# A quarter of the gate products moved from VectorE to ScalarE and GpSimd, with a new order of the experts' halves and own tables for one unit

## The chip, the core and the metric

The kernel runs on one core of a Trainium2 chip. A core has TensorE (PE: matmuls, with a weight load PEld that overlaps them), VectorE (DVE), ScalarE (ACT), GpSimd (POOL) and SyncE (SP, which issues DMAs). Each engine executes its own instructions in order; engines wait for one another by semaphores. The metric is the device time of one execution in microseconds (us). Before the change it is 1290.98 us, the median of 3 runs (1289.37 to 1291.66).

## The reference, cut to what matters

The input is 2 batches of 1024 tokens of 128 values. Four blocks are each added to the residual:

```
x = x + attention+MLP, 2 layers      (block 1)
x = x + local attention+MLP, 2 layers (block 2)
x = x + local and latent attention   (block 3)
x = x + experts(layernorm(x))        (stage D)
```

Block 2 has 8 heads of 64. Queries and keys are l2-normed, scaled, and rotated with per-position tables: `q * cos * scale + rotate_half(q) * sin * scale`, and for k with the inverse scale. The kernel holds the products of the position tables with the learned scales in tiles `tab`.

Stage D has 64 experts of 32 hidden values, all computed for all 2048 tokens, and a routing that masks the scores:

```
scores = softmax(x @ Wr + br)                  # 2048 x 64
order  = argsort(-scores, axis=0)              # tokens of each expert
group  = sorted.reshape(32, 64, 64).sum(1)     # sums of 64 ranks
mask   = the 512 best of the 2048 groups, put back in token order
fs     = where(mask, scores, 0) / (sum + 1e-6)
h      = silu(x @ Wup + bup) * (x @ Wgate + bgate) * fs
out    = h @ Wdown + fs @ bdown
```

## The kernel before

All four stages run in one program. In blocks 1 to 3 and stage D the order of PE, ACT, DVE and POOL instructions is written by hand: each engine gets its instructions as the Python code emits them. Blocks 1 and 2 use a `Pipe`: `later(n, f, rank)` puts `f` n beats ahead, and within a beat the lower rank comes first.

**Block 2** (`BlockB`) has 32 units (2 layers, 2 batches, 8 tiles of 128 positions), one in every 8 beats. A unit projects q and k to PSUM (`queries`, L714) and v (L719), squares and sums (L723, L736), takes the root (`root`, L742), and scales q and k into the tile `raw` (`scale`, DVE, L748 to L752). On POOL follow `cross` (L761: two products of the swapped halves with the sine table, into `t2`) and `straight` (L768: the product with the cosine table, in place); `both` adds them (L775, on POOL, but on DVE for the first unit). Transposes on PE and copies on ACT make `qT` and `kT` (L807, L809), and the scores follow (L822), their maximum, exponential, product with v, and a quarter-wise MLP.

The first unit's opening steps (`clear`, `turn`, `copy`, `queries`, `square`, `sums`, `root`, `scale`) are handed to block 1 (`first`, L554), whose last group of tokens emits them among its own work (`BlockA.after`, L425). Block 2's pools reuse the memory of block 1's pools. The scale-and-position tables of all 8 tiles are built by `tables` on POOL: for layer 0 the four parts for tiles 0 to 3 in beat 0 with the rank -2, those for tiles 4 to 7 from beat 20 on; they take their tiles from block 2's pool `b2`. Block 1's tile `hid` (512 hidden values of its MLP) is in its pool `a1`. The input norm of the following 512 tokens (`prep`, `norm`: statistics on DVE L641, root on POOL L645 to L648, product on ACT L652) is set for beat 6 for the first of them.

**Stage D.** The 64 experts give 32 units of 128 hidden rows x 512 tokens x 2, so 64 halves. A half is: the up matmul (128x512, `matmul`, L1652, into a PSUM bank `big`), a silu on ACT (L1661) into `hid`, the gate matmul (L1652), and on DVE one operation `hid = (gate + bias) * hid` (L1675), here called the gate. `Experts` keeps lists of ups and of gates to be made and a queue `ready` of gates whose matmul is emitted. `feed` keeps 3 gates in `ready` (4 once no up is left), `fill(n)` retires n gates, and after each emits one up and feeds. The last two halves' `hid` lies in the expert input `xT` itself (L1645).

`route` computes the mask on DVE and calls `fill` between its steps, so that matmuls, silus and gates run beside it: 

- 36 items of sort passes over parts of the scores that block 3 left over (`front.todo`); up to two gates in three items, one in two at the end
- ten passes over 1024 values, each a max and a min (L1511, L1512), with one gate after each
- the exchange of the two batches' halves through two DMAs, one issued by SP, one by ACT (L1841, L1842), with four gates and two subtractions (L1816) while they run; L1848 takes what they bring
- four passes, a gate after each; then the sign (L1858), the sums of 64 (L1862), their broadcast to all partitions by 16 PE transposes and 4 ACT copies (L1869, L1870), a minimum (L1871), three gates
- five rounds of a search (L1883 to L1895; the compare of 2048 values with a running sum is L1886), one gate in each
- the tail: four short chains that go DVE, PE, DVE (L1904, L1917, L1937, L1947) with three gates beside each, two compares over all scores (L1961, L1962), the rest of the gates, and the scan (L1969)

After the scan come the masks and the down matmuls (L1727), which need all halves.

Of the kernel before, what the change touches and what calls it, by code (L numbers as in the profile page):

```python
# [28 lines left out]
P = 128  # L29
# [3 lines left out]
MT = S // P  # L33
# [144 lines left out]
class BlockA:  # L178
# [11 lines left out]
    def __init__(self, k, es, nxt):  # L190
# [4 lines left out]
        self.p3 = es.enter_context(k.tc.tile_pool(name="a3", bufs=3))  # L195
        self.pipe = Pipe()
# [228 lines left out]
    def after(self, l, b, g, st):  # L425
# [6 lines left out]
        hid = self.p1.tile([P, 4, 512], F32, tag="hid", name=k.name("hid"))  # L432
# [106 lines left out]
class BlockB:  # L539
# [14 lines left out]
    def first(self):  # L554

        out = self.out = {}
        out["clear"], out["turn"], out["copy"] = self.features(0, 0, 0)
# [18 lines left out]
    def run(self):  # L576
        pipe = self.pipe
        self.tables(0)
        for n in range(1, 4):
            pipe.later(32 * n - (26 if n == 1 else 32), lambda n=n: self.prep(0, n % 2, n // 2, 1))  # L580
# [31 lines left out]
    def tables(self, l):  # L612
# [3 lines left out]
        for i, n in ((1, "b_qksr"), (0, "b_qks")):  # L616
            dst = self.p2.tile([P, MT, 2, 64], F32, tag=f"tab{i}", name=k.name("tab"))
            for j in range(2):
                for m in (slice(0, MT), ) if l else (slice(0, 4), slice(4, MT)):
                    sc = k.row(n, (l * 2 + j) * 64, 64)[:, None, :].to_broadcast([P, m.stop - m.start, 64])  # L620
                    self.pipe.later(
                        (2 if l else 5 * m.start) + 2 * j + 4 * (1 - i) if l or m.start else 0,
                        lambda dst=dst, i=i, j=j, m=m, sc=sc: nc.gpsimd.tensor_tensor(
                            dst[:, m, j, :], k.b_tab[:, m, 2 * i + j, :], sc, ALU.mult
                        ),
                        rank=3 if l or m.start else -2,
                    )
            out.append(dst)
        self.tabs[l] = out[::-1]

# [73 lines left out]
    def project(self, l, b, m, later):  # L704
        k, nc, st = self.k, self.k.nc, self.st[l][b]
        first = (l, b, m) == (0, 0, 0)
        t = st.setdefault("first", {}) if first else {}

# [48 lines left out]
        def cross():  # L757
            t2 = t["t2"] = self.p2.tile([P, 2, 8, 64], F32, tag="t2", bufs=1, name=k.name("t2"))
            r4 = t["raw"].rearrange("p (j h) d -> p j h d", j=2)
            for a, z in ((0, 32), (32, 0)):  # L760
                nc.gpsimd.tensor_tensor(  # L761
                    t2[:, :, :, a : a + 32], r4[:, :, :, z : z + 32],
                    self.tabs[l][1][:, m, :, None, a : a + 32].to_broadcast([P, 2, 8, 32]), ALU.mult,
                )

        def straight():
            r4 = t["raw"].rearrange("p (j h) d -> p j h d", j=2)
            nc.gpsimd.tensor_tensor(  # L768
                r4, r4, self.tabs[l][0][:, m, :, None, :].to_broadcast([P, 2, 8, 64]), ALU.mult
# [845 lines left out]
class Experts:  # L1615
# [39 lines left out]
    def up(self, n=1):  # L1655

        now = [(unit, e, self.matmul(unit, e, self.k.d_up)) for unit, e in self.ups[:n]]
# [8 lines left out]
    def feed(self):  # L1666

        while self.gates and len(self.ready) < (3 if self.ups else 4):
            unit, e = self.gates.pop(0)
            while (unit, e) in self.ups:  # L1670
# [3 lines left out]
            self.ready.append(  # L1674
                lambda ps=ps, hd=hd, bias=bias: self.k.nc.vector.scalar_tensor_tensor(  # L1675
                    hd, ps, bias, hd, ALU.add, ALU.mult
                )
            )

    def fill(self, n=1):  # L1680

        for _ in range(n):
            if self.ready:
                self.ready.pop(0)()
                self.up()
                self.feed()
# [109 lines left out]
def route(k, p1, front, fill):  # L1796
# [25 lines left out]
    for n, f in enumerate(front.todo):  # L1822
# [6 lines left out]
        fill(n % 2 if left < 10 else n % 3 > 0)  # L1829
# [395 lines left out]
```

## Time and profile before

| quantity | value |
| --- | --- |
| median of 3 runs | 1290.98 us |
| profiled execution | 1289.73 us, span 1287.9 us, mean clock 0.97 |
| block 1 | 0 to 341.8 us |
| first scores of block 2 (L822) | 357.29 us |
| stage D: last block of passes handed over, to the start of the ten long passes | 1067.60 to 1118.85 us |
| ten long passes and exchange, to L1848 | 1118.85 to 1142.04 us |
| merge and sums, to the first L1886 | 1142.04 to 1156.30 us |
| search, to L1894 | 1156.30 to 1173.57 us |
| tail, to the scan | 1173.57 to 1193.78 us |
| scan, masks, down matmuls | 1193.78 to 1287.9 us |

How to read the profile. It is one execution. The first lines give busy time and share of each engine; "the chain that ended last" follows the last instruction back through what released it. A row of a timeline has the start, the duration, the engine, the line of the kernel, the operation, `out<-in`, the tile's shape, the count of merged records, and in brackets the idle time of the engine before it with what ended that. A DVE row can last a little longer than the distance to the next row: instructions overlap at their ends, so what one costs in a chain is that distance, the slot. A 128x512 float32 matmul leaves two records. Windows give each engine's busy time in a stretch, with the clock that TensorE was granted.

### The profile page before, as it was taken

Reading aid. Unit: us, or ns where it says so; the run is one execution under the profiler, and the core shown is the slowest. Engines: PE = TensorE matmul, PEld = TensorE weight load, DVE = VectorE, ACT = ScalarE, POOL = GpSimd, SP = SyncE. Lnnn points to the kernel's source line nnn. Section 1 sums busy time; section 2 is a strip of 40 time slices with the busy share of each in tenths; the row PEclk is TensorE's granted clock in tenths of the full one; section 3 lists DMA queues with packets and bytes.
Section 4 is the critical chain, followed back from the end, with each engine's and each line's share of the span. In section 5 each row is a group of like instructions: output and inputs, shape, how many; then the busy total and the mean of one; then the engine's idle time right before and its main releaser. Section 6 shows DMA issues by size and latency. Waiting matters only on the chain.

```text
span 1287.9 us, 23417 instructions
## 1 busy us (share of the span) xinstructions
PE 1142.3 (89%) x9381; PEld 738.6 (57%) x9441; DVE 867.5 (67%) x1789; ACT 642.8 (50%) x1209; POOL 478.8 (37%) x556
## 2 busy tenths in 40 slices
PE   5899999999578999999989867989998978998798
PEld 3566666666345666666666634555555543343688
DVE  5566666554477776776776625556568989998763
ACT  5454545444355765665655635656766754342000
POOL 2523333232488786676786542212122210000000
PEclk9999999999899999999999988989999989999799
DMA  9000000000001100010100002000000000000000
GB/s 297 1 1 1 1 1 1 2 1 1 17 18 26 27 22 18 22 26 18 26 22 18 5 16 103 2 1 2 2 1 1 2 1 1 0 17 0 25 17 18
DMA packets 19841, 25.18 MB, mean 20 GB/s; under 512 B 2762, under 2 KB 13716, under 8 KB 19476
## 3 DMA queue, kind: packets, MB, share of 16 engines
q1 hardware_dynamic: 19076, 23.02, 6.3%
q8 instruction: 75, 1.23, 0.4%
q10 hardware_dynamic: 656, 0.66, 0.2%
q14 instruction: 34, 0.28, 0.1%
HBM read 13.32 MB, written 1.05 MB: 11 GB/s over the span
## 4 chain that ended last, share of the span: by engine, by line
PE 39%; DVE 20%; ACT 7%; issue 4%; POOL 3%; DVEq 0%; POOLq 0%; ACTq 0%
PE mm L1727 5%; PE bank L947 4%; PE big L1652 4%; PE s L714 3%; PE s L822 3%; PE s L1249 2%; PE bank L867 2%; PE tr L1286 2%; DVE nm L1254 2%; DVE r_zab L1511 2%; DVE r_zab L1512 2%; PE s L1245 2%; DVE hid L1675 2%; DVE rinv L736 2%; PE bank L964 1%
## 5 line engine op out<-in xcount | busy, mean ns | idle before, releaser
L1254 DVE TENSOR_REDUCE nm<-s 128x4 f32<-128x1024 f32 (+1 forms) x64 | 71.0, 1151 | 59.1 <-PE s L1249 59.0
L377 DVE TENSOR_REDUCE nm<-s 128x1 f32<-128x1024 f32 x64 | 75.1, 1215 | 51.7 <-PE s L371 51.7
L761 POOL TENSOR_TENSOR t<-raw,tab 128x512 f32<-128x512 f32 x64 | 79.7, 1268 | 77.1 <-DVE raw L752 73.0
L1287 ACT COPY pT<-tr 128x512 f32<-128x512 f32 x120 | 70.0, 598 | 69.5 <-PE tr L1286 69.2
L1661 ACT ACTIVATE hid<-big,cols 128x512 f32<-128x512 f32 x62 | 42.0, 687 | 75.6 <-PE big L1652 75.5
L1286 PE MATMUL tr<-ident,pr 128*128 128x128 f32 x480 | 77.6, 285 | 2.2 <-ACT pT L1287 1.8
L768 POOL TENSOR_TENSOR raw<-raw,tab 128x1024 f32<-128x1024 f32 x32 | 75.5, 2360 | 2.4
L723 ACT ACTIVATE sq<-s 128x1024 f32<-128x1024 f32 x32 | 32.8, 1025 | 85.7 <-PE s L714 85.7
L383 ACT ACTIVATE pr<-s,nm 128x1024 f32<-128x1024 f32 x64 | 71.1, 1122 | 7.7 <-DVE nm L377 7.6
L775 POOL TENSOR_TENSOR raw<-raw,t 128x1024 f32<-128x1024 f32 x31 | 73.3, 2365 | 1.7
L394 PEld LDWEIGHTS bank<-ident,pr 128*128 128x128 f32 x512 | 56.2, 141 | 30.0 <-issue 22.5
L406 PE MATMUL bank<-pT,v 128*64 128x128 f32 x1024 | 72.5, 286 | 0.7 <-DVE pT L399 0.2
L1652 PE MATMUL big<-xTd,d_gate 128*128 128x512 f32 x128 | 66.2, 609 | 7.7 <-DVE hid L1675 3.9
L1652 PE MATMUL big<-xTd,d_up 128*128 128x512 f32 x128 | 68.7, 627 | 2.3 <-DVE r_above L1891 2.3
L406 PEld LDWEIGHTS bank<-pT,v 128*64 128x64 f32 x1024 | 57.2, 141 | 22.4 <-issue 11.4
L397 ACT COPY pT<-bank 128x512 f32<-128x512 f32 x64 | 34.9, 588 | 68.2 <-PE bank L394 68.2
L1286 PEld LDWEIGHTS tr<-ident,pr 128*128 128x128 f32 x480 | 54.9, 145 | 20.8 <-issue 11.5
L371 PE MATMUL s<-kk,q 64*128 64x512 f32 x256 | 64.7, 615 | 0.6 <-ACT pr L383 0.5
L394 PE MATMUL bank<-ident,pr 128*128 128x128 f32 x512 | 65.2, 276 | 0.0
L714 PE MATMUL s<-b_wqkv,hT 128*128 128x512 f32 x128 | 63.8, 622 | 1.3 <-ACT hT L682 1.3
L1727 PEld LDWEIGHTS mm<-d_down,hid 128*128 128x128 f32 x496 | 60.4, 194 | 5.7 <-DVE xo L1758 1.9
L1727 PE MATMUL mm<-d_down,hid 128*128 128x128 f32 x496 | 61.1, 278 | 1.3 <-DVE xo L1758 1.3
(363 smaller groups left out, 2792.1 us busy)
## 6 DMA issues: line engine op xcount, KB each, us to landing
vs<-v SPq DMA_DIRECT2D x60, 130.0 KB, 2.2
b_wqkv<-in_L_ffn_wqkv_dram SPq DMA_DIRECT2D x2, 768.0 KB, 8.9
b_tab<-in_c_xpos_dram SPq DMA_DIRECT2D x1, 1024.0 KB, 8.0
d_up<-in_L_ffn_Wup_dram SPq DMA_DIRECT2D x1, 1024.0 KB, 5.8
d_gate<-in_L_ffn_Wgate_dram SPq DMA_DIRECT2D x1, 1024.0 KB, 7.5
out_dram<-xo SPq DMA_DIRECT2D x3, 256.0 KB, 2.3
rows<-in_rows_dram SPq DMA_DIRECT2D x1, 760.0 KB, 7.0
b_w<-in_L_ffn_w_dram SPq DMA_DIRECT2D x2, 341.0 KB, 7.2
```

The source lines that it names most:

```text
L377: nc.vector.tensor_reduce(t["nm"][h], t["s"][h], AX.X, ALU.max, negate=True)
L383: nc.scalar.activation(t["pr", h], t["s"][h], AF.Exp, bias=t["nm"][h], accum_out=st["sums"][:, h, qt % 4 : qt % 4 + 1],)
L394: nc.tensor.transpose(ps[:, i * P : (i + 1) * P], t["pr", h][:, at : at + P], k.ident)
L406: nc.tensor.matmul(t["u"][h * 64 : h * 64 + 64, :P], v[:, kb, h * 64 : h * 64 + 64], t["pT"][:, h, kb], start=(kb == 0), stop=(kb == MT - 1),)
L714: nc.tensor.matmul(qk[:, cut], lhsT, k.b_wqkv[:, l, cut], start=True, stop=True)
L761: nc.gpsimd.tensor_tensor(t2[:, :, :, a : a + 32], r4[:, :, :, z : z + 32], self.tabs[l][1][:, m, :, None, a : a + 32].to_broadcast([P, 2, ...
L768: nc.gpsimd.tensor_tensor(r4, r4, self.tabs[l][0][:, m, :, None, :].to_broadcast([P, 2, 8, 64]), ALU.mult)
L775: eng.tensor_tensor(flat, flat, t["t2"].rearrange("p j h d -> p (j h d)"), ALU.add)
L1254: nc.vector.tensor_reduce(nm[h], view[h], AX.X, ALU.max, negate=True)
L1286: nc.tensor.transpose(ps[:, c * P : (c + 1) * P], pr[:, c, t * P : (t + 1) * P], k.ident)
L1652: self.k.nc.tensor.matmul(ps, weights[:, rows], self.xT[:, cut], start=True, stop=True)
L1727: nc.tensor.matmul(sums[part][:, cols], hid[tp, h, c][:, e, cols], k.d_down[:, c + 8 * e, :], start=start and e == 0, stop=False,)
```

## The change

- `Experts.feed` marks the gate that is emitted when one more than a multiple of four gates are left. For a marked gate (an "aside") ACT writes `gate + bias` from PSUM to an SBUF tile, and POOL multiplies it into `hid`. The SBUF tile takes the tag `c_xn` of a pool with one buffer for it, so an ACT write waits for the POOL product before.
- `fill(n, ups)` counts only gates on DVE; asides are retired in passing. After each retired gate `ups` ups are emitted, and `up` emits none while two or fewer are left and more than 32 gates are left (those last ups write into the expert input).
- `route` passes `ups=2` up to the search. Gates on DVE: one in every second item of `todo`, after every second long pass, one in the exchange and one for each of the two subtractions, after every second pass of the merge, one instead of three ahead of the search, four instead of one in each of its rounds, one instead of three in the tail's steps (by then none is left).
- In block 2 the first unit has own tables, `tab_own`, made by two POOL products in `clear`, inside block 1, in a pool that outlasts it. The general tables of layer 0 are set for beat 7 with the rank 3 (tiles 0 to 3) and beat 20 on (tiles 4 to 7).
- Block 1's `hid` gets its own pool `a4`.
- The first `prep` goes from beat 6 to beat 10.

In the counts of gates on DVE and asides, by stage, before and after (the built programs): first stage 23 / 18 and 6; long passes 10 / 5 and 1; exchange 4 / 3 and 1; merge 4 / 2 and 1; ahead of the search 3 / 1 and 0; search 5 / 19 and 7; tail 15 / 0. Matmuls of `L1652` in the first stage: 49 / 75.

```
+        self.p4 = es.enter_context(k.tc.tile_pool(name="a4", bufs=1))
...
-        hid = self.p1.tile([P, 4, 512], F32, tag="hid", name=k.name("hid"))
+        hid = self.p4.tile([P, 4, 512], F32, tag="hid", name=k.name("hid"))
...
-        out["clear"], out["turn"], out["copy"] = self.features(0, 0, 0)
+        clear, out["turn"], out["copy"] = self.features(0, 0, 0)
+        own = self.own = self.p0.tile([P, 2, 2, 64], F32, name="tab_own")
+        out["clear"] = lambda: (clear(), self.table_of(own, 0, slice(0, 1)))
...
-            pipe.later(32 * n - (26 if n == 1 else 32), lambda n=n: self.prep(0, n % 2, n // 2, 1))
+            pipe.later(32 * n - (22 if n == 1 else 32), lambda n=n: self.prep(0, n % 2, n // 2, 1))
...
+                    at = 2 + 2 * j + 4 * (1 - i) if l else 20 + 2 * j + 4 * (1 - i) if m.start else 7
                     self.pipe.later(
-                        (2 if l else 5 * m.start) + 2 * j + 4 * (1 - i) if l or m.start else 0,
-                        lambda dst=dst, i=i, j=j, m=m, sc=sc: nc.gpsimd.tensor_tensor(
+                        at, lambda dst=dst, i=i, j=j, m=m, sc=sc: nc.gpsimd.tensor_tensor(
...
-                        rank=3 if l or m.start else -2,
+                        rank=3,
...
+    def table_of(self, dst, l, m):
+        k, nc = self.k, self.k.nc
+        for i, n in ((1, "b_qksr"), (0, "b_qks")):
+            nc.gpsimd.tensor_tensor(
+                dst[:, i], k.b_tab[:, m, 2 * i : 2 * i + 2, :].rearrange("p m j d -> p (m j) d"),
+                k.row(n, l * 128, 128).rearrange("p (j d) -> p j d", d=64), ALU.mult,
+            )
...
+        tab = lambda i: self.own[:, i] if first else self.tabs[l][i][:, m]
...
+        if len(self.ups) <= 2 and len(self.gates) > 32:
+            return
         now = [(unit, e, self.matmul(unit, e, self.k.d_up)) for unit, e in self.ups[:n]]
...
+            self.ready.append((len(self.gates) % 4 == 1, ps, hd, bias))
+
+    def gate(self, aside, ps, hd, bias):
+        nc, k = self.k.nc, self.k
+        if aside:
+            t = k.wpool.tile([P, 512], F32, tag="c_xn", name=k.name("aside"))
+            nc.scalar.activation(t, ps, AF.Identity, bias=bias)
+            nc.gpsimd.tensor_tensor(hd, hd, t, ALU.mult)
+        else:
+            nc.vector.scalar_tensor_tensor(hd, ps, bias, hd, ALU.add, ALU.mult)
+
+    def fill(self, n=1, ups=1):
+        while n and self.ready:
+            now = self.ready.pop(0)
+            self.gate(*now)
+            self.up(ups)
+            self.feed()
+            n -= not now[0]
...
-        fill(n % 2 if left < 10 else n % 3 > 0)
+        fill(n % 2, 2)
...
         sort_pass(k, za, zb, 1024, j, j == 512)
-        fill()
+        fill(j.bit_length() % 2, 2)
...
-    fill(2)
+    fill(1, 2)
     for _ in range(2):
         next(second)
-        fill()
+        fill(1, 2)
...
         sort_pass(k, za, zb, 1024, j, False)
-        fill()
+        fill(j.bit_length() % 2, 2)
...
     nc.vector.tensor_reduce(gm, z3, AX.X, ALU.min)
-    fill(3)
+    fill(1, 2)
...
         nc.vector.tensor_scalar(junk, every, piv, None, ALU.is_gt, ALU.add, accum_out=above)
-        fill()
+        fill(4)
...
-    fill(3)
+    fill(1)
```

More of the change, by code (lines that the diff above doesn't have):

```diff
@@ L618, in tables @@
             for j in range(2):
-                for m in (slice(0, MT), ) if l else (slice(0, 4), slice(4, MT)):
+                for m in (slice(0, MT),) if l else (slice(0, 4), slice(4, MT)):
                     sc = k.row(n, (l * 2 + j) * 64, 64)[:, None, :].to_broadcast([P, m.stop - m.start, 64])
+                    at = 2 + 2 * j + 4 * (1 - i) if l else 20 + 2 * j + 4 * (1 - i) if m.start else 7
                     self.pipe.later(
-                        (2 if l else 5 * m.start) + 2 * j + 4 * (1 - i) if l or m.start else 0,
-                        lambda dst=dst, i=i, j=j, m=m, sc=sc: nc.gpsimd.tensor_tensor(
+                        at, lambda dst=dst, i=i, j=j, m=m, sc=sc: nc.gpsimd.tensor_tensor(
                             dst[:, m, j, :], k.b_tab[:, m, 2 * i + j, :], sc, ALU.mult
                         ),
-                        rank=3 if l or m.start else -2,
+                        rank=3,
                     )
@@ L762, in cross @@
                     t2[:, :, :, a : a + 32], r4[:, :, :, z : z + 32],
-                    self.tabs[l][1][:, m, :, None, a : a + 32].to_broadcast([P, 2, 8, 32]), ALU.mult,
+                    tab(1)[:, :, None, a : a + 32].to_broadcast([P, 2, 8, 32]), ALU.mult,
                 )
@@ L768, in straight @@
             nc.gpsimd.tensor_tensor(
-                r4, r4, self.tabs[l][0][:, m, :, None, :].to_broadcast([P, 2, 8, 64]), ALU.mult
+                r4, r4, tab(0)[:, :, None, :].to_broadcast([P, 2, 8, 64]), ALU.mult
             )
@@ L1673, in feed @@
             bias = self.k.col("d_bgate", unit[2] + 8 * e)
[L1674 to L1686, printed above, removed]
+            self.ready.append((len(self.gates) % 4 == 1, ps, hd, bias))
[14 more added lines that the diff above has]
+            n -= not now[0]
 def stage_d(k, out, front, ex):
@@ L1919, in route @@
     nc.tensor.matmul(ps[:, 18:34], k.mat["blk"], eq, start=True, stop=True)
-    fill(3)
+    fill(1)
     cs = new([P, 34], "cs")
@@ L1937, in route @@
     nc.tensor.matmul(ps[:, :1], k.mat["pair"], cnt[:, 0:1], start=True, stop=True)
-    fill(3)
+    fill(1)
     num = new([P, 1], "num")
@@ L1950, in route @@
     v = new([P, 1], "v")
-    fill(3)
+    fill(1)
     both = junk[:, :P]
```

## The prediction

> **What bounds the kernel now.** I read the page first, then the waits, then a table of windows by stage, then the timelines of the two places that the change touches. The page's busy shares and its chain of waits:
>
> ```profile
> PE 1142.3 (89%) x9381; PEld 738.6 (57%) x9441; DVE 867.5 (67%) x1789; ACT 642.8 (50%) x1209; POOL 478.8 (37%) x556
> ...
> PE 39%; DVE 20%; ACT 7%; issue 4%; POOL 3%; DVEq 0%; POOLq 0%; ACTq 0%
> ```
>
> PE leads on average, but an average hides stages. The windows of the routing part, from 1067.60 to the scan at 1193.78 (columns: window, length, busy PE, PEld, DVE, ACT, POOL, clock, DMA share, GB/s):
>
> ```profile
> 1067.60:1118.85 51.25, 46.51 (x96) 16.18 (x96) 49.72 (x160) 17.55 (x27) 0.00 (x0) 1.00 0.00 0
> 1118.85:1142.04 23.19, 23.05 (x50) 8.21 (x51) 22.64 (x38) 8.53 (x13) 0.00 (x0) 1.00 0.10 24
> 1142.04:1156.30 14.26, 13.97 (x45) 6.80 (x44) 14.00 (x23) 7.73 (x14) 0.00 (x0) 1.00 0.00 1
> 1156.30:1173.57 17.27, 12.94 (x28) 4.61 (x26) 16.85 (x31) 5.48 (x8) 0.46 (x1) 1.00 0.00 0
> 1173.57:1193.78 20.21, 17.57 (x50) 8.34 (x50) 16.66 (x50) 3.44 (x5) 0.64 (x2) 1.00 0.01 1
> ```
>
> They are: first sort passes, long sort with the exchange, merge, search, tail. DVE is busy nearly throughout, POOL idle, ACT a third: here DVE's order sets the time, so taking 16 gates from DVE is aimed rightly. But PE is almost as full in the first three rows, and the change gives PE more to do there. The price of one 128x512 matmul comes from rows of a gapless stretch:
>
> ```profile
> 1139.85 1.02 PE L1652 MATMUL big<-xTd,d_gate 128*128 128x512 f32 x2
> ...
> 1151.09 1.13 PE L1652 MATMUL big<-xTd,d_up 128*128 128x512 f32 x2
> ```
>
> Thirteen matmuls (each recorded as two) start in those 11.24 us: 0.865 us each. A gate on DVE takes a slot of 0.66 us (L1675 at 1118.19, the next operation at 1118.85).
>
> **Stage D, part by part.** The order of both builds gives the counts; halves total 64 in each. Before, the five windows plus the first passes hold 23 gates, then 10 beside the long sort, 4 in the exchange, 4 in the merge, 3 before the search, 5 in it and 15 in the tail. Afterwards 48 stay on DVE: 18, 5, 3, 2, 1, 19, 0; the 16 others are an ACT Identity from PSUM plus a POOL product. PE does 75 matmuls in the first stage instead of 49.
>
> *First stage.* DVE alone: 51.25 less 23 x 0.66 plus 18 x 0.66 = 47.95 us, end at 1115.6. PE executes in order, and each retired gate emits two ups and one gate: the gate that DVE needs last stands behind 63 matmuls (21 retired gates x 3). From 1070.25, where the first up starts, that is 63 x 0.865 = 54.5, plus about 2.2 us in which the first ups wait for a free bank (such a wait shows before: the gate at 1072.47 waited 1.20 for DVE) and 0.74 for the gate: 1127.7, against 1118.85. **+8.9.** Behind each late gate stand the sort passes on DVE, all later ones with them.
>
> *Long sort.* Before 1118.85 to 1136.81. Now ten passes of 1.20 (two rows of 0.60), 4 gates on the path 2.64, and some 1.2 of waiting while PE catches up: 15.9, end at 1143.6; total **+6.8**.
>
> *Exchange.* Before, 5.23 us from the last pass to L1848, which waited for ACT's half of the transfer, issued at 1138.21 and landed 3.83 later. ACT's queue now has two silus ahead of that issue, each behind PE; what waits behind it are the later silus, which nobody needs yet. Bounds 4.5 to 6.5 us; I take 5.2, so it stays **+6.8**, less 0.3 of slack: +6.5.
>
> *Merge and sums.* L1848 1.26, four passes 4.80, 2 gates 1.32, then sign 0.77 and sum 1.15. The broadcast of the sums (16 transposes, 4 ACT copies ending at 1156.0, begun when the sum ended at 1152.67) takes 3.5 and was covered by one reduction and three gates; now by the reduction and one gate, so it shows. 12.8 instead of 14.26: **+5.0 to +5.3**.
>
> *Search.* 14 more gates x 0.66 = 9.2: **+14.5**. PE has 22 gates x 0.865 = 19 us to do in 26, and no ups.
>
> *Tail.* Before 20.21: 15 gates (9.9), DVE's own small operations and two 1.28 scans over sT (6.9), and waits for PE, the largest of which the waits list as:
>
> ```profile
> DVE hid L1675 <- PE big L1652: 2.9, 4, 1.0
> ```
>
> Afterwards only the serial chain is left: 6.9 + four hops over PE, 2.3, + 0.5 because PE, now idle, slows (the clock reads 0.52 in 1193.78 to 1198, once the matmuls stop). 9.7 in all: **-10.5**. Stage D: 14.5 - 10.5 = **+4.0**. Behind the scan nothing differs. Bounds: the search cannot begin before PE has done the 96 matmuls of the stages ahead of it, less 3 that may still be queued: 1070.25 + 2.2 + 93 x 0.865 + 0.74 = 1153.6, then 26.5 of search and 9.7 of tail end at 1189.8, which is -4; +8 if the bank waits and the exchange reach their far ends.
>
> **The port of DVE and POOL.** POOL's product is a two-input operation of 128x512 (the row of that size, L761, has a mean of 1268 ns). What such a thing does to DVE shows elsewhere:
>
> ```profile
> 1035.70 0.47 DVE L1511 TENSOR_TENSOR r_zab<-r_zab 128x256 f32<-128x256 f32 x1
> 1036.09 0.85 DVE L1512 TENSOR_TENSOR r_zab<-r_zab 128x256 f32<-128x256 f32 x1
> ...
> 354.48 1.28 DVE L749 SCALAR_TENSOR_TENSOR e<-e,rinv 128x16 f32<-128x16 f32 x1
> ```
>
> The first two are twins; only the second lies beside a POOL product (1035.98 to 1036.66). The third, normally 0.17, lasted as long as POOL's 1.26 us addition beside it. Sort passes are of the kind that suffers. Of 16 products 6 fall where DVE waits for PE, 7 beside gates fed from PSUM or the one-input compare of the search (a PSUM-fed DVE row at 360.25 kept its 1.22 beside a POOL product), 1 in the exchange's wait. Two meet a pass: 2 x 0.43 = **+0.9**; bounds 0 and 5 x 1.27 = 6, the upper needing nearly every one after the first stage to hit.
>
> The Trainium skill speaks against this edit: "GPSIMD Engine Reference", section "8. Key points", says that POOL shares its SBUF interfaces with VectorE and contends with DVE instructions that have two SBUF inputs. The rows above agree. Read alone, with every product stopping a pass for 1.27 us, it would put +20 us on the sum; by the rows and places it is 0.9.
>
> **Block 2's opening.** The first unit's path:
>
> ```profile
> 339.56 1.23 DVE L752 TENSOR_TENSOR raw<-s,y 128x1024 f32<-128x1024 f32 x1
> ...
> 349.61 1.23 DVE L775 TENSOR_TENSOR raw<-raw,t 128x1024 f32<-128x1024 f32 x1 [7.38 <-POOL raw L768]
> ```
> ```profile
> 341.85 2.78 POOL L623 TENSOR_TENSOR tab<-b_tab,rows 128x256 f32<-128x256 f32 x4 [4.09 <-PE bank L487]
> 344.59 2.48 POOL L761 TENSOR_TENSOR t<-raw,tab 128x512 f32<-128x512 f32 x2
> ...
> 347.23 2.35 POOL L768 TENSOR_TENSOR raw<-raw,tab 128x1024 f32<-128x1024 f32 x1
> ```
> ```profile
> 354.55 1.65 ACT L652 ACTIVATE xi<-xo,ln_mn,ln_rs 128x128 f32<-128x128 f32 x4 [0.31 <-POOL ln_mn L648]
> 356.11 0.56 ACT L809 COPY qT<-bank 128x512 f32<-128x512 f32 x1
> ```
> ```profile
> 357.29 1.65 PE L822 MATMUL s<-kT,qT 64*64 64x128 f32 x32 [3.52 <-ACT kT L809]
> ```
>
> `raw` is ready at 340.79, yet the cross starts at 344.59: POOL first waits 4.09 us for block 1's last matmul, whose memory the tables take, and then builds them. Own tables, built inside block 1 (two 128x128 products on POOL, which idles there 4.09 us), and the separate pool for `hid` let the cross start at about 340.85: 3.7 earlier. The sum (L775) then ends near 347. A second delay goes: the norm of the next 512 rows, four beats later now, no longer stands ahead of the copies on ACT (it began 354.55, the copies could follow only at 356.11). POOL's four parts of the general tables (2.78), displaced behind the cross, and xo's 1.26 are late next; scores come at 350 to 351 instead of 357.29, -6 to -7. From there a unit starts its scores every 10.6 us (357.29, 369.15, 379.89, 390.52), bound by its own work, so the lead lasts, less what the shifted norm takes from the second unit (it delays DVE by up to 1.65). Bounds: -3.7 (the cross alone) and -8; taken **-6.5**, nearest to the first scores.
>
> **Sum.** -6.5 + 4.0 + 0.9 = -1.6. The profiled execution took 1289.73 (span 1287.9, 1.8 around it): 1288.1. It lies 1.25 below the median of 1290.98, so **1289.4**.
>
> **Rivals.** 0.2% is 2.6 us, about what a measurement of this kernel can tell from no change.
>
> *Slower: PE's order in the first stage costs more.* Place: the stage up to 1118.85; price: each 0.01 us on a matmul slot is 0.63, each bank wait comes on top. It decides once the last gate there ends after 1131.9, 4.2 later than worked out. For it: the second up needs a bank that DVE or ACT has to free, and the third matmul of every retired gate waits behind both; clock slices of 8 tenths occur on the page. Against: gapless rows of 0.865 at full clock. About +5, 1296; chance 0.25.
>
> *Faster: the gain of the 16 gates is kept.* What DVE loses to PE in the first stage it makes good by the search, stage D ends between -1 and -4, say -2.5, block 2 gives its 6.5: -9, and with half of the port's price -8.5, 1282.5. For it: 16 x 0.66 = 10.6 us leave DVE, and 3.5 us of waits the tail. Against: 54.5 us of matmuls don't fit into the 45.4 that DVE would leave them (1070.25 to 1115.6), and every later gain is counted already. 0.18.
>
> *Block 2's lead is lost* before its end, to POOL (14.95 busy in the first 19.2 us) or at a transfer: 0 + 4.9, 1295.9. Against: regular units. 0.07.
>
> *It doesn't do what it says*: excluded by the built order, which has 48 gates on DVE.
>
> **Numbers.** Forecast 0.50, own range 1285.5 to 1293.5, half of it faster by over 0.2%, half within. Slower rival 0.25, faster 0.18, lost lead 0.07 (0.05 of it within 0.2%, its lead being lost in part). Faster 0.25 + 0.17 = 0.42; within 0.25 + 0.01 + 0.05 = 0.31; slower 0.25 + 0.02 = 0.27. The range reaches down to the faster rival and up to the slower two: 1282 to 1296.5; stage D's and block 2's far bounds, each taken with the other's likely value, lie within it but for a fraction (-4 and -6.5 with 0.9: 1281.4; +8 and -6.5: 1293.4; +4 and -8: 1287.9).
>
> **What would show it.** In the changed profile: DVE waiting some 12 us for PE's `big` in the first stage, which ends near 1127.7 less block 2's lead; the compare of the first search round 5 later than 1156.30 on the same basis; the tail 10 us long; sort rows stretched beside POOL products; the first cross at 340.9, first scores at 350 to 351, and the same lead at the end of block 2. Wrong it is if the first stage is not PE's, or if the lead is gone by the second dozen of units.

## The result, and the profile after

The changed kernel takes 1293.91 us, the median of 20 runs (1290.92 to 1297.75); the kernel before, run beside it, 1291.14 (20 runs). The ratio is 1.0025, with a 95% interval from 1.0014 to 1.0037: slower by 3.2 us by the ratio (the medians differ by 2.8), where the prediction had -1.6 and gave 0.27 to slower. The profiled execution of the changed kernel took 1290.92 us (span 1289.1), 3.0 below its median; its executions spread more than those of before, and part of the explanation lies in that. Line numbers of the changed kernel are higher: the matmul helper is L1665, the gate L1698, the aside L1695 (ACT) and L1696 (POOL), the cross L774, the scores L835, the search's compare L1908.

The page's busy shares hardly differ from those of before:

```profile
PE 1141.5 (89%) x9381; PEld 742.9 (58%) x9441; DVE 867.8 (67%) x1773; ACT 653.2 (51%) x1225; POOL 501.4 (39%) x574
...
PE 57%; DVE 25%; ACT 7%; POOL 5%; issue 5%; DMA 0%; DVEq 0%; POOLq 0%; ACTq 0%
```

DVE has 16 gates fewer and is exactly as busy as before (867.8 against 867.5 us). That line alone should make a reader stop: 10.6 us of work went away and did not leave the sum. The chains of the two pages can't be set side by side: the shares printed for the one of before add up to 73% of its span, for this one to 99%. The windows of stage D, in the five stages of the prediction (same columns as there):

```profile
1061.58:1121.54 59.96, 58.70 (x135) 24.88 (x136) 51.73 (x155) 34.19 (x52) 6.50 (x5) 1.00 0.00 1
1121.54:1142.58 21.04, 20.26 (x48) 8.76 (x47) 20.02 (x32) 11.35 (x18) 4.34 (x3) 1.00 0.12 26
1142.58:1157.69 15.11, 10.93 (x28) 5.29 (x26) 12.49 (x18) 2.94 (x6) 1.70 (x1) 0.66 0.00 0
1157.69:1185.29 27.60, 20.78 (x45) 7.85 (x44) 27.17 (x46) 4.68 (x7) 9.80 (x9) 1.00 0.00 0
1185.29:1195.11 9.82, 2.83 (x13) 2.16 (x13) 6.57 (x35) 0.00 (x0) 0.12 (x1) 0.64 0.00 0
```

PE fills the first stage (58.7 of 60 us), has fewer matmuls than it could do in the third (10.9 of 15.1), and there its clock reads 0.66. The waits of DVE in these stages, longest first:

```profile
DVE hid L1698 <- PE big L1665: 6.8, 6, 2.4
DVE r_zab L1908 <- ACT r_every L1892: 2.4, 1, 2.4
DVE r_cs L1944 <- PE mm L1941: 1.0, 1, 1.0
DVE r_num L1962 <- PE mm L1959: 0.7, 1, 0.7
```

The third and fourth are the tail's hops, which no gate covers now. The second is new. The prediction's merge term did let the broadcast of the sums show, but at the 3.5 us that it took before.

The opening of block 2, POOL, then DVE, ACT and PE:

```profile
341.20 2.50 POOL L774 TENSOR_TENSOR t<-raw,tab_own 128x512 f32<-128x512 f32 x2 [3.20 <-DVE raw L765]
...
343.86 2.36 POOL L781 TENSOR_TENSOR raw<-raw,tab_own 128x1024 f32<-128x1024 f32 x1
346.17 3.79 POOL L626 TENSOR_TENSOR tab<-b_tab,rows 128x256 f32<-128x256 f32 x4
```
```profile
346.26 1.73 DVE L788 TENSOR_TENSOR raw<-raw,t 128x1024 f32<-128x1024 f32 x1 [3.79 <-POOL raw L781]
```
```profile
349.73 0.57 ACT L822 COPY qT<-bank 128x512 f32<-128x512 f32 x1
...
353.97 1.65 ACT L664 ACTIVATE xi<-xo,ln_mn,ln_rs 128x128 f32<-128x128 f32 x4 [3.18 <-POOL ln_mn L660]
```
```profile
351.48 0.92 PE L835 MATMUL s<-kT,qT 64*64 64x128 f32 x12 [0.76 <-POOL kT L810]
```

The cross starts at 341.20 instead of 344.59, the copies at 349.73 instead of 356.11, now ahead of the norm's product, and the scores at 351.48 instead of 357.29. The DVE sum lasted 1.73 us instead of 1.23: beside it POOL builds the general tables.

To compare kernels whose earlier parts end at different times, the rest of this text measures stage D from its first gate on DVE to the scan, each stage as the difference of two start times in the traces (the search here ends with the operation behind L1894, 0.2 us later than in the windows):

| kernel | to the long passes | long passes, exchange | merge | search | tail | sum |
| --- | --- | --- | --- | --- | --- | --- |
| before | 47.2 | 23.2 | 14.3 | 17.5 | 20.0 | 122.1 |
| changed | 55.8 | 21.0 | 15.1 | 27.8 | 9.7 | 129.4 |
| the same, one up in the first stage | 49.3 | 23.8 | 17.7 | 30.6 | 10.2 | 131.6 |
| the same, no POOL product | 55.4 | 20.9 | 13.7 | 26.7 | 10.1 | 126.8 |
| the same, no asides | 44.4 | 21.3 | 12.9 | 27.3 | 21.1 | 127.0 |
| the same, PE busy in the merge | 55.8 | 21.0 | 14.3 | 28.1 | 9.8 | 129.0 |
| old order, every fourth gate aside | 48.9 | 24.4 | 14.9 | 17.5 | 20.2 | 125.9 |
| old order, asides from the search on | 47.2 | 23.2 | 14.3 | 17.7 | 18.9 | 121.2 |
| the same, one gate beside each hop | 47.2 | 23.4 | 14.3 | 17.7 | 16.9 | 119.5 |

These sums repeat to 0.3 us: stage D as changed has 129.4, 129.3, 129.3 and 129.1 in four traces of kernels that are alike there, as before 122.1, 121.9, 122.1, 121.8 and 121.9 in five.

### The profile page after: what moved, and what is told of

The parts are those of the page before. It is cut to its first block, busy times and chain, and to the rows that moved or that the text cites. A ratio compares the mean times of both kernels' runs of the same rounds, so it can differ in the third digit from the quotient of the medians.

```text
span 1289.1 us, 23422 instructions
## 1 busy us (share of the span) xinstructions
PE 1141.5 (89%) x9381; PEld 742.9 (58%) x9441; DVE 867.8 (67%) x1773; ACT 653.2 (51%) x1225; POOL 501.4 (39%) x574
## 3 DMA queue, kind: packets, MB, share of 16 engines
q8 instruction: 75, 1.23, 0.4%
## 4 chain that ended last, share of the span: by engine, by line
PE 57%; DVE 25%; ACT 7%; POOL 5%; issue 5%; DMA 0%; DVEq 0%; POOLq 0%; ACTq 0%
PE mm L1749 5%; PE big L1665 4%; PE bank L407 4%; PE s L372 4%; PE bank L960 4%; PE s L727 3%; PE s L835 2%; PE s L1262 2%; PE bank L880 2%; PE bank L467 2%; DVE nm L1267 2%; PE bank L488 2%; DVE nm L378 2%; PE tr L1299 2%; PE bank L395 2%
## 5 line engine op out<-in xcount | busy, mean ns | idle before, releaser
L774 POOL TENSOR_TENSOR t<-raw,tab 128x512 f32<-128x512 f32 x62 | 77.2, 1266 | 74.7 <-DVE raw L765 71.7
L1665 PE MATMUL big<-xTd,d_gate 128*128 128x512 f32 x128 | 64.1, 619 | 9.5 <-DVE hid L1698 8.6
L407 PEld LDWEIGHTS bank<-pT,v 128*64 128x64 f32 x1024 | 55.8, 138 | 22.4 <-issue 11.0
L1665 PE MATMUL big<-xTd,d_up 128*128 128x512 f32 x128 | 62.6, 611 | 2.0 <-DVE hid L1698 1.2
L1271 ACT ACTIVATE pr<-s,nm 128x256 f32<-128x256 f32 (+1 forms) x160 | 61.1, 470 | 2.0 <-DVE nm L1267 1.5
```

Source lines behind the costliest of these rows:

```text
L407: nc.tensor.matmul(t["u"][h * 64 : h * 64 + 64, :P], v[:, kb, h * 64 : h * 64 + 64], t["pT"][:, h, kb], start=(kb == 0), stop=(kb == MT - 1),)
L774: nc.gpsimd.tensor_tensor(t2[:, :, :, a : a + 32], r4[:, :, :, z : z + 32], tab(1)[:, :, None, a : a + 32].to_broadcast([P, 2, 8, 32]), AL ...
L1665: self.k.nc.tensor.matmul(ps, weights[:, rows], self.xT[:, cut], start=True, stop=True)
```

## The experiments

The kernel before ran beside each group of kernels. Its own median there lay between 1290.42 and 1293.09, so a time is compared with the runs beside it, by the ratio.

**The changed kernel again, and its two halves.** Three kernels: the changed one without an edit; block 2's edits with the old stage D; stage D's edits with the old block 2.

> The changed kernel once more, beside the kernel before on the same chip. Its profile put block 2's lead at 5.1 us and stage D's loss (from the lead at the first gate, 6.0, to the scan) at 7.3 us. If that is the whole story, the time is 1 to 2 us above the kernel before. The rival is that a second group of executions near 1296.5 (about half of the 20 runs on record, at a mean clock of 0.960 instead of 0.966) belongs to the changed kernel alone: then the median comes out 3 to 6 above.

Measured: 1294.41 (ratio 1.0034, 1.0022 to 1.0046).

> Only block 2's edits (own tables, own pool, later prep), stage D as before. If block 2's lead of 5.1 us lasts to the end, 5 us faster than before (1286). If the lead is lost to the spread of the clock in block 3, between 0 and 2 faster. If the second group of slower executions comes from block 2's edits, some runs are about 5 above the rest here too.

Measured: 1287.70 against 1290.53, ratio 0.9979 (0.9967 to 0.9991): 2.8 faster, between the two cases.

> Only stage D's edits (asides, two ups, four gates a round), block 2 as before. If stage D loses what the profile shows, 6 to 8 us slower than before (1298). The prediction's sum for stage D with the port was 4.9 (1296). If the slower group comes from stage D's edits, half of the runs lie 5 above the rest.

Measured: 1297.39, ratio 1.0055 (1.0042 to 1.0068): 6.9 slower. Six runs lay between 1296.06 and 1299.17, so stage D's edits show no group of their own in these six. The halves add up, -2.8 + 6.9 = +4.1 against +3.9 for the whole, measured beside them: no interaction between them shows. Stage D loses 7.2 (129.3 less 122.1), and block 2 gives less than its lead.

**One up in the first stage.**

```
-        fill(n % 2, 2)
+        fill(n % 2)
```

> The changed kernel with one up instead of two for each gate in the first sort passes, two afterwards as before. Theory: there PE's order (three matmuls for each retired gate) holds DVE up, 8 us in all, and PE then falls idle in the merge and slows. With two matmuls a gate DVE sets that stage, it ends near 1110.5 instead of 1121.5, PE has 16 to 20 matmuls more to do afterwards and stays busy in the merge; the gain is 7 to 10 us against the changed kernel: 1283 to 1286. Rival: PE's total is what counts, and what is put off returns as waits in the long passes and the exchange: within 2 us of the changed kernel.

Measured: 1298.51, ratio 1.0063 (1.0041 to 1.0085), slower than the changed kernel. The theory fell, and the rival's mechanism, put more strongly than it was, took its place. The first stage did get 6.5 shorter (49.3), but all of it and more came back: the merge is 2.6 longer, the search 2.8, the exchange's stage 2.8. DVE's longest wait and the window of PE ahead of the search tell where:

```profile
DVE r_zab L1908 <- ACT r_every L1892: 5.4, 1, 5.4
```
```profile
1152.00:1163.77 11.77, 11.47 (x39) 5.72 (x38) 6.29 (x11) 8.38 (x15) 1.63 (x1) 1.00 0.00 0
```

PE is busy 11.5 of 11.8 us there, at full clock. The matmuls that were put off stand in PE's queue ahead of the transposes that broadcast the sums, and the whole search waits for these. So two ups early were not a mistake in itself: in this order PE's matmuls ahead of the search have to be done somewhere, and DVE met them either way. (Of the 4.1 us by which the median is above the changed kernel's, stage D holds 2.2. In this run's trace the first gate comes 4.1 us later than in the trace of the changed kernel run beside it: there is a difference ahead of stage D as well, which the last experiments take up.)

**No product on POOL.**

```
             nc.scalar.activation(t, ps, AF.Identity, bias=bias)
-            nc.gpsimd.tensor_tensor(hd, hd, t, ALU.mult)
```

> The changed kernel without POOL's product in the asides: ACT still writes gate plus bias, but nothing multiplies it into hid, so a quarter of the halves lack their gate factor. In the changed kernel's trace nine DVE operations beside such a product last 7.27 us longer than their twins, 2.86 of it behind the first stage. Theory (the port costs about 3 us on the path, the rest falls into waits for PE): 2.5 to 4 us faster than the changed kernel. The prediction's 0.9 would leave it within 1 us. If all of it is on the path, 7.

Measured: ratio 1.0006 to the kernel before (0.9985 to 1.0027), median 1292.97; the interval is too wide to set it against the changed kernel, but the trace tells what stage D does: it is 126.8 instead of 129.4, so the 16 products cost 2.6 us on the path: 1.4 in the merge, 1.1 in the search, 0.5 in the first stage, where PE bounds anyway, and 0.4 given back in the tail. This is the theory's 2.5 to 4, at its lower end. Two of the stretched rows of the changed kernel, DVE, and the products beside them, POOL:

```profile
1143.84 1.64 DVE L1524 TENSOR_TENSOR r_zab<-r_zab 128x512 f32<-128x512 f32 x1
...
1173.90 1.25 DVE L1914 SCALAR_TENSOR_TENSOR r_n<-r_n,r_above 128x1 f32<-128x1 f32 x1
```
```profile
1143.23 1.70 POOL L1696 TENSOR_TENSOR hid<-hid,aside 128x512 f32<-128x512 f32 x1 [0.80 <-ACT aside L1695]
...
1173.87 1.27 POOL L1696 TENSOR_TENSOR hid<-hid,aside 128x512 f32<-128x512 f32 x1 [3.43 <-ACT aside L1695]
```

The first normally lasts 0.68, the second, an operation on 128 numbers, 0.16. A DVE operation with two inputs in SBUF that begins while POOL's product runs doesn't end before the product has ended. The one that comes second waits: where such an operation of DVE was already running, it kept its time, and the product lasted 1.65 and 1.70 us instead of 1.27 (the row at 1143.23). The search, which the prediction took for safe, has such tiny operations between its compares.

**PE kept busy in the merge.** After each of the merge's four passes:

```
+    def warm(z):
+        ps = k.tr()
+        for i in range(4):
+            nc.tensor.transpose(ps[:, i * P : (i + 1) * P], z[:, i * P : (i + 1) * P], k.ident)
...
+        warm(zb)
```

> The changed kernel with four extra 128x128 transposes on PE after each of the merge's four passes (their output is read by nobody). In the changed kernel PE's granted clock is 0.55 to 0.59 from 1146 to 1158, after it ran out of matmuls, and the search then waits 2.44 us for the broadcast of the sums. Theory: kept busy, PE has the full clock there and the wait shrinks to 1 us or less: 1.5 to 2.5 us faster than the changed kernel. Rival: the broadcast is a chain of PE and ACT hops whose length doesn't hang on the clock, or the extra transposes stand ahead of it: no gain, or up to 1 us slower.

Measured: 1296.12, ratio 1.0031 (1.0014 to 1.0049), no faster than the changed kernel. The clock did what the theory says; window ahead of the search and wait of this kernel:

```profile
1152.00:1158.00 6.00, 3.51 (x16) 1.92 (x16) 5.51 (x10) 0.00 (x0) 0.00 (x0) 1.00 0.00 0
```
```profile
DVE r_zab L1915 <- ACT r_every L1899: 1.2, 1, 1.2
```

With the clock at 1.00 the wait halves, 2.4 to 1.2, and the merge takes 0.8 less; the extra transposes make one pass wait 0.45, and the search gave back 0.3. In sum 0.4 is won in stage D (129.0), hardly more than the 0.3 to which these sums repeat. The half clock is real, and worth 1.2 us here, no more. In the changed kernel it comes after a wait of PE; PE's rows around it:

```profile
1139.74 5.31 PE L1665 MATMUL big<-xTd,d_gate 128*128 128x512 f32 x12
1148.12 2.08 PE L1665 MATMUL big<-xTd,d_gate 128*128 128x512 f32 x2 [3.06 <-DVE hid L1698]
...
1153.22 3.81 PE L1891 MATMUL tr<-ident,r_gs 128*128 128x128 f32 x16
```

After 3.06 us of idling the same matmul leaves 2.08 instead of 1.02 in its row, and sixteen transposes take 3.81. The Trainium skill, "TensorE: Matmul & The Clock Gate", section "Part 1: The HAM clock gate", says that about 3.4 us of idling halve the clock and that as long a busy stretch restores it. The second agrees here: PE is busy again from 1153.22, and the clock is full from 1157.3. The first doesn't: the whole wait is 3.06 us, and the clock already falls at 1147.1, 2.1 us into it.

**No asides, new order.**

```
-            self.ready.append((len(self.gates) % 4 == 1, ps, hd, bias))
+            self.ready.append((False, ps, hd, bias))
```

> The changed kernel with no aside at all: all 64 gates on DVE, two ups a gate up to the search, four gates in each round, the rest in the tail. Theory: in the order of before each aside was a loss of 0.4 to 0.5 us; here nine of the 16 met a sort pass, 7.3 us in all, while 16 x 0.66 = 10.6 us come back to DVE, and the first stage has 18 retired gates instead of 24 and so fewer matmuls to wait for: within 2 us of the changed kernel. Rival (the asides carry what gain there is, the order loses): 4 us or more slower than the changed kernel. Rival (the asides are the loss): 3 us or more faster.

Measured: 1293.18, ratio 0.9999 to the kernel before (0.9983 to 1.0014). Stage D takes 127.0: 2.4 less than with asides, though DVE has 16 gates more. So the theory (within 2 us) was near, and on the side of the third case, which the ratio meets (0.9999 against 1.0025 and 1.0034 with asides, some 3 to 5 us): the asides are a loss, in stage D of 2.4, and the new order is one of 4.9 (127.0 less 122.1). The first stage is 44.4, shorter than with asides: without them 18 gates are retired there and not 24, and 16 fewer of the matmuls that held DVE up start there in the trace. The order's loss is in waits that the old order doesn't have: DVE of this kernel,

```profile
DVE hid L1698 <- PE big L1665: 3.3, 5, 1.0
DVE r_zab L1870 <- DMA r_zab<-r_zab: 1.3, 1, 1.3
DVE r_zab L1908 <- ACT r_every L1892: 1.1, 1, 1.1
```

and 1.3 more in the tail, 7.0 in all; with the old order they are 3.4 (2.9 for PE, 0.5 other): 3.6 of the 4.9.

**Old order, every fourth gate aside.** Block 2's edits, stage D as before, each fourth gate on ACT and POOL in its old place (`gate` as in the change):

```
-                self.ready.pop(0)()
+                self.gate(*self.ready.pop(0))
...
+            self.ready.append((len(self.gates) % 4 == 1, ps, hd, bias))
```

> Block 2's edits, stage D in the order of before (one up a gate, same places, 15 in the tail), but each fourth gate aside and counted like any other: 16 gates leave DVE and nothing else moves. If the asides are sound and only the new order costs, DVE saves 16 x 0.66 = 10.6 us less 3 to 5 of stretched operations, and PE, which then has 116 us to do in about 119, gives some of it back in waits: 3 to 7 us faster than block 2's edits alone (1281 to 1285 where these take 1287.7). Rival: PE bounds stage D whatever DVE does: within 1.5 us of block 2's edits alone.

Measured: 1287.91, ratio 0.9979 (0.9957 to 1.0001), just that of block 2's edits alone, but stage D is 3.8 longer (125.9). The theory fell: DVE loses 10.6 us of gates and wins nothing. Of this kernel two rows of DVE, and the sums over its stage D, ahead of those of the kernel without asides:

```profile
1114.64 1.64 DVE L1524 TENSOR_TENSOR r_zab<-r_zab 128x512 f32<-128x512 f32 x1
...
1123.11 1.76 DVE L1525 TENSOR_TENSOR r_zab<-r_zab 128x512 f32<-128x512 f32 x1
```
```profile
sum 125.91, PE 112.34 PEld 43.27 DVE 116.89 ACT 51.46 POOL 21.75; mean PE 22.47 PEld 8.65 DVE 23.38 ACT 10.29 POOL 4.35
```
```profile
sum 121.91, PE 110.39 PEld 42.78 DVE 116.01 ACT 42.10 POOL 1.10; mean PE 22.08 PEld 8.56 DVE 23.20 ACT 8.42 POOL 0.22
```

DVE is busy 116.89 us with 48 gates and 116.01 with 64. An aside among sort passes takes a slot of 0.66 from DVE and adds 0.95 to 1.08 to the pass beside it (0.6 in one of nine cases). Eleven operations lasted longer, by 10.1 us in all, nearly the 10.6 that the 16 gates gave back. The stage is longer by waits of DVE for PE and ACT: 6.3 us, against 3.4 without asides.

**Asides only where they do little harm.** Block 2's edits with the first prep at beat 6, old order, every second gate aside from the search on, asides not counted; and then the same with the tail's gates spread out:

```
+            self.ready.append((len(self.gates) < 20 and len(self.gates) % 2 == 1, ps, hd, bias))
...
+            n -= not now[0]
```
```
-    fill(3)
+    fill(1)
```

> Block 2's edits with the prep at beat 6; stage D in the old order with one up a gate, no asides up to the search, and from there on every second gate aside, asides not counted: each round of the search then retires one gate on DVE and one aside, the tail 10 gates instead of 15, half of them asides. Theory: an aside among the two-input sort passes saves DVE 0.66 us and costs it about 1.1 by the port, so it loses; beside the one-input compare and gates fed from PSUM it costs DVE next to nothing, so 10 asides there save 5 to 8 us against the same kernel without them (1286.3): 1278 to 1281. Rival: the search and the tail hang on PE and on the chain, and DVE's saved time turns into waits: within 2 us of 1286.3. Other rival: the port costs the same there: slower.

Measured: 1286.15, ratio 0.9944 (0.9922 to 0.9965). Stage D is 121.2, 0.9 less than without: the first rival. The search hardly grows (17.7), so the products cost next to nothing there, but the tail waited:

```profile
DVE hid L1696 <- PE big L1665: 2.7, 4, 1.3
DVE hid L1696 <- PE tr L1923: 1.9, 1, 1.9
DVE xTd L1696 <- ACT aside L1693: 1.3, 1, 1.3
```

> The kernel with asides only from the search on, with one gate on DVE instead of three beside each of the tail's four hops over PE. In the run with three, ten gates crowded into the first two hops and the tail took 18.9 us: DVE waited 6 us for PE and for the asides there. Theory: spread out, two gates (one of them aside) lie beside each hop, PE's 10 matmuls (8.7 us) fit beside the chain, and the tail takes 11 to 13 us: 5 to 7 us faster than with three, that is 0.8 to 1.0% faster than the kernel before. Rival: the tail is bound by the chain of asides (ACT, then POOL, one buffer) or by the last gates ahead of the scan: within 2 us of the run with three (0.56% faster than before).

Measured: 1283.37 against 1291.57, ratio 0.9937 (0.9913 to 0.9961). The tail takes 16.9, 2.0 less, which is the rival's case and not the 5 to 7 of the theory; stage D 119.5, 2.6 below the order of before. This ratio is the lowest of all kernels here, and the kernel is faster than the one before and the changed one; its interval overlaps that of block 2's edits with the early prep (0.9952, below), ahead of which the sums put it by 2.6. Of what the theory missed, one wait of 1.9 is for the tail's first transpose, behind matmuls in PE's queue. Another part is the products again: in the tail four small operations of DVE with two inputs in SBUF lie beside one and last 2.8 us longer in all. Two of them, normally 0.23 and 0.16:

```profile
1179.33 1.06 DVE L1951 SCALAR_TENSOR_TENSOR r_eq<-r_inc,r_tot,r_eq 128x16 f32<-128x16 f32 x1
...
1183.43 1.12 DVE L1975 TENSOR_TENSOR r_v<-r_v,r_none 128x1 f32<-128x1 f32 x1
```

**Where block 2's lead goes.** Block 2's edits with the prep back at beat 6, and the kernel before with the prep at beat 10:

```
-            pipe.later(32 * n - (22 if n == 1 else 32), lambda n=n: self.prep(0, n % 2, n // 2, 1))
+            pipe.later(32 * n - (26 if n == 1 else 32), lambda n=n: self.prep(0, n % 2, n // 2, 1))
```

(for the second kernel the other way round, and nothing else).

> Block 2's edits without the move of the first prep (it stays at beat 6), stage D as before. By the prediction the norm's product then stands ahead of the copies of q and k on ACT: of the first scores' 5.8 us of lead, the cross's 3.4 stay. If that holds to the end the time is 2 us above that of all of block 2's edits. Rival: the prep's place costs the second unit what it gives the first: no difference.

Measured: 1286.33 against 1291.35, ratio 0.9952 (0.9936 to 0.9969).

> The kernel before with one edit: the first prep at beat 10 instead of 6. By the prediction the norm's product leaves ACT free for the copies of q and k, so the first scores come up to 2 us earlier and the whole up to 2 us faster. By the comparison of the two block 2 kernels (with the move 2.7 us faster than before, without it 5.0) the move costs about 2 instead. A rival says that both numbers are the lottery of the clock's half-speed windows: no difference beyond 1 us.

Measured: 1288.32 against 1293.09, ratio 0.9964 (0.9950 to 0.9978).

Each half of block 2's edits alone is worth 0.4 to 0.5%, both together 0.2%. Neither theory foresaw that. The intervals exclude that the two gains add up (0.84% against at most 0.33%); that both together are worth less than one alone they don't show, since they touch or overlap. Inside block 2 the traces are regular: measured at the maximum of the scores (L828 before), and from the same point at block 1's end, the lead is 2.1 to 3.0 us with one half and, from the third unit on, 4.8 to 5.7 with both, and steady to 0.5 us within each trace up to the last unit but one. Behind that it is not. At the last unit all thirteen traces with an edit in block 2 lose 1.2 to 1.3 us, the three without none. The clock there, in the changed kernel and, 5 us later, in the kernel before:

```profile
716.00:720.00 4.00, 3.79 (x21) 3.80 (x22) 0.87 (x5) 2.27 (x5) 3.73 (x4) 0.63 0.00 0
```
```profile
721.00:725.00 4.00, 3.61 (x26) 3.11 (x27) 0.96 (x5) 3.29 (x7) 3.77 (x4) 1.00 0.00 0
```

and it falls there in all thirteen and in none of the three. But this loss comes back: the kernel before has half-clock stretches too, and at 963 the lead is 5.7 to 6.1 us in all nine traces with both halves. What separates them comes behind that. Five lose 1.6 us by 987, four of these 3.1 more by 999, and at stage D's first gate the lead is 6.2 us in four, 3.9 in one, and 0.3 to 0.7 in four.

**PE kept busy at block 3's end.** I first put the difference down to a stretch of half clock at 1050 to 1060, and bridged the idle time ahead of it, in the changed kernel and in the one before:

```
             eng.tensor_tensor(local, local, remote, ALU.add)
+            if last:
+                ps = k.mm()
+                for i in range(8):
+                    at = i % 4 * P
+                    nc.tensor.transpose(ps[:, at : at + P], k.ident, k.ident)
```

> The changed kernel with eight extra 128x128 transposes on PE in block 3's last step, where PE otherwise waits 2.4 us for the mixing (their output is read by nobody). In the traces of the changed kernel's variants the first gate comes 6.2 us early where the clock in 1050 to 1060 stays above 0.8, and only 0.3 to 0.7 us early where it falls to 0.56 to 0.6. Theory: the clock's half-speed stretch at the end of block 3 makes the two groups of executions and takes part of block 2's lead; bridged, the stretch is rare, the upper group goes and the median falls by 2 to 4 us against the changed kernel (1290 to 1292). Rival: the half-speed stretches fall elsewhere as well, the spread stays, and the median moves by less than 1 us.

> The same eight transposes in the kernel before. Its profile has a clock of 0.56 and 0.76 from 1050 to 1060. If the stretch is the same in both kernels, it gains as much as the changed kernel (2 to 4 us), and the change's cost is untouched by it. If block 2's lead was what moved the changed kernel into the stretch more often, the kernel before gains less than 1 us.

Measured: 1295.55, ratio 1.0032 (1.0020 to 1.0044), and 1289.56, ratio 0.9998 (0.9984 to 1.0012). Nothing moved in either, and the clock in 1050 to 1055 still read 0.57 in the changed kernel: eight transposes, 1.04 us, were not enough to hold it. So the run doesn't test the stretch, but its trace shows that the theory had the wrong place: the lead, 4.5 us up to the maximum at 984, was 1.3 at the next, at 996 (and 0.6 at the first gate). Windows of PE in this kernel, then in the changed kernel's own profile:

```profile
988.00:992.00 4.00, 3.34 (x28) 2.22 (x27) 3.33 (x8) 2.66 (x6) 0.89 (x2) 0.65 0.00 0
992.00:996.00 4.00, 4.00 (x24) 2.36 (x24) 1.87 (x4) 0.00 (x0) 2.49 (x3) 0.50 0.00 0
```
```profile
988.00:992.00 4.00, 3.79 (x39) 2.52 (x40) 3.75 (x10) 1.50 (x3) 2.51 (x4) 1.00 0.00 0
992.00:996.00 4.00, 4.00 (x50) 2.86 (x47) 3.77 (x8) 2.90 (x8) 0.93 (x1) 1.00 0.01 4
```

PE is fully busy in both from 992 to 996, at a clock of 0.50 in the one and 1.00 in the other. The same half-clock stretch, beginning between 989 and 992, stands in all four traces whose lead ends at 0.3 to 0.7 and in none of the other twelve. That such stretches eat the lead is thus shown; why PE falls into them in one execution and not in the next, and more often with block 2's edits, is not. The traces give one hint. In each of the sixteen, half-clock stretches begin only on a grid of 3.413 us, to 0.01, and last whole multiples of it (but for a last one that the trace's end cuts off). In the changed kernel's they begin at 717.0, 744.3, 781.9, 853.6 and 962.8: 8, 11, 21 and 32 steps apart. So a shift of 2 to 5 us puts other work into a step. Of the nine traces with both halves, in the four with a lead of 6.2 block 1's last addition on DVE (L513 before) begins 0.3 to 0.6 us behind an edge of the grid, in the other five 0.8 to 1.2 us. No run sets that distance, so that it decides is not shown. The clock's mean over the runs points to block 2 as well: it is 0.971 in 11 of 22 runs of the kernel before, and in 1 of 12 of block 2's edits alone beside them, with no edit in stage D.

## Why the prediction was wrong

Its steps in order, in the changed kernel's trace from the first gate on.

*First stage, +8.9*: right. 55.8 against 47.2 is +8.7, and without POOL's product still 55.4: PE bounds it. *Long passes and exchange, -2.4*: measured -2.2; the exchange's wait stayed under 1 us. *Tail, -10.5*: -10.4. Those three terms are right to 0.3 us, and with them the reading that three matmuls for a retired gate hold DVE up.

*Merge, -1.5 (12.8)*: wrong by 2.3: 15.1. The step "now by the reduction and one gate, so it shows" took the broadcast at its old length, 3.5 us at full clock. PE, ahead with its matmuls, idled, and the broadcast ran at half clock: from the end of the sum to the first compare it is 4.6 us (1153.08 to 1157.69). The extra transposes show 1.2 us of wait for that. One stretched pass adds 1.0.

*Search, +9.2*: 10.3, of which 1.1 is one stretched tiny operation between two compares; without the product it is 9.2.

*The port, +0.9*: the step "Two meet a pass: 2 x 0.43" failed twice over. Nine operations were stretched, not two, by 0.4 to 1.1 each, 7.27 us in all. Five of them lie in the first stage, which PE bounds; 2.6 us reached the path, and the 1.0 and 1.1 above are part of them. The row chosen for the price (0.43, beside a product of 0.68 us) was the cheapest of the two shown; the other said that the DVE operation lasts until POOL's has ended, and that is what the runs show. The place was misjudged too: the search is not only one-input compares and gates. "16 x 0.66 = 10.6 us leave DVE" was true and worthless: 48 gates and 64 cost DVE the same.

So stage D is +7.3 where 4.9 was worked out.

*Block 2, -6.5*: the mechanism was right at the start, the step "so the lead lasts" was not. The cross came 3.4 earlier (3.7 worked out), the first scores 5.8 (6 to 7), and from the third unit on the lead was about 5, less by what the shifted norm was to give back (up to 1.65). But the median of block 2's edits alone is -2.8, below the lower bound of 3.7 that the cross alone was to give. Up to stage D's first gate the lead lasts in four traces of nine (6.2 us); in the others 1.6 or 4.7 us of it go in half-clock stretches of block 3. How many of all executions lose it the traces can't say, nor why those do.

Together: -2.8 + 6.9 = +4.1 in the runs of the halves, +3.2 in the result. The forecast's -1.6 was off by 3.7 from block 2 and by 2.4 from stage D, which makes +4.5; the 1.3 between that and the result are a difference between sets of runs. The result is that of the rival on the slower side in sign only: its mechanism, a stage beyond 1131.9, did not occur (1121.5 with a lead of 6). The rival "block 2's lead is lost", at 0.07, names the larger part of what did.

## What to carry to other kernels

Before work is moved to an idle engine, ask what it shares with the engine that it relieves: here POOL's product held up every DVE operation with two inputs in SBUF that began beside it, and an aside of 0.66 us cost about 1 us of stretch, while beside one-input or PSUM-fed operations it was nearly free (the search grew by 0.2). When matmuls are pulled ahead, look for what stands behind them in the in-order queue, and for the place where PE then runs dry: one shows as a wait for a broadcast, the other as a half clock. A lead won early in a kernel should not be booked in full against a median: measure it at several later points, beside the clock, in more than one execution.

## What the runs showed that was not expected

- A DVE operation on 128x1 numbers with two inputs in SBUF lasted 1.25 us instead of 0.16 beside a POOL product of 1.27 us.
- Two gains of 0.4 to 0.5% in the same place gave 0.2% together. In the traces TensorE's clock halves, for whole steps of 3.41 us, at other places once its work is shifted by 2 to 5 us: 1.2 to 1.3 us were lost in every shifted trace at the end of block 2 and won back later, 1.6 and 3.1 us were lost in some in block 3.
- Sixteen transposes spread over the merge, with PE idle for at most 1.6 us at a time, held the clock at 1.00; eight together, 1.04 us, ahead of a wait of 1.55 us in block 3 did not. There PE was busy for 1.39 of the 3.41 us ahead of the fall (1047.33 to 1050.74).
